# Attention block with compacted tokens: transfers regrouped, a row added to the reciprocals, buffers added

## The chip, the cores and the metric

The kernel runs on one core of a Trainium2 chip. The metric is the device time of one execution in microseconds (us). TensorE is called PE, VectorE DVE, ScalarE ACT, GpSimd POOL and SyncE SP, as in the profile.

## The reference

For each of 16 batches, with x of 512 features by 1024 tokens and a 0/1 mask over the tokens:

```python
xt = jnp.transpose(x, (0, 2, 1))
q = xt @ Wq.T                                   # 8 heads of 64
scores = scale * jnp.einsum('bhqd,bhkd->bhqk', qh, qh)
logits = (scores * cmask + (1.0 - cmask) * NEG) * rmask
attn = jax.nn.softmax(logits, axis=-1)
ctx = jnp.einsum('bhqk,bhkd->bhqd', attn, qh)
out = ctx @ Wo.T
return x + jnp.transpose(out, (0, 2, 1))
```

Queries, keys and values are one and the same projection. A masked query row has all logits zero, so its result is the mean of the values of all 1024 tokens. An unmasked row attends to unmasked tokens only.

## The kernel before, in words

For each batch the kernel works on C = 544 slots that hold the unmasked tokens (384 to 544 of them, which the kernel tests): four blocks of 128 and a tail of 32. Rows are fetched by gathers on POOL's queue (`rows`) and written back by scatters on it (`scatter_now`). Masked rows receive the mean of the values, added in `rest` (L742).

One batch goes through these steps. `xt` transposes the gathered rows on PE into a PSUM buffer `pm` (two of them) and splits them into two 16-bit parts (ACT L352, DVE L353). `query` projects (L414), ACT copies the result to `q` (L417), and DVE zeroes unused slots (L420). `qsplit` splits q of one pair of heads into a high part h and a low part l in the tile `hl` (L428, L429) and sends them by SP's queue into `xx`: for each head, the lower 64 partitions hold h and l, the upper ones l and h, so that one matmul over 128 rows sums two products. That takes six transfers a pair (L432 to L437), four pairs a batch. `value` transposes q to token order (L457, ACT L459, squares L448); `value_tail` does it for the tail (L474, DVE L477, which frees the `pm` buffer). `scores` multiplies xx with itself (L566), ACT takes the exponential with a row sum z (L570); the tails of four heads are done together (`i is None`, L545 to L560), and their high and low parts go to `pt` in four transfers. `attend` multiplies the exponentials by the values (L583, tails L586) and ACT copies the sum to `c` (L590).

`recip_sums` makes reciprocals of the row sums of a pair in columns of `rcol`: four blocks for each of two heads, and, for every second pair, a ninth column with the tail sums of four heads (zt). `recip_rows` transposes them (L620), DVE copies them to `rr` (L623), SP sends `rr` to a DRAM tile `rd` (L626) and from there, spread over 64 partitions each, into `rb`: per head 512 columns (L630) and 32 tail columns (L633), four transfers. `norm` multiplies c by rb (L655), adds means (L656) and splits the product into `ch` and `cl` (L658, L659) and the tail (L660, L661). `project` multiplies by the output weights (L671), DVE adds the row (`plus`, L676), and a scatter sends it.

The means need row sums of x in its own layout: `load_half` loads 128 x 512 pieces into two buffers `xm` by SP's queue (L337), eight a batch, and `sum_half` sums each on ACT (L343).

`run` sets the order. A batch has 18 steps (16 pairs of heads and blocks, and two tail steps); each step issues scores, then the functions due in `free`, then a share of the list `m`, which holds the next batch's `xt`, `query`, `value` and the last batch's `project`. `norm` of pair p is due five steps after the pair's last block; for pair 2 that is the batch's last step. Pair 3 follows in the next batch's list. This program order is a priority: a scheduler then orders each engine's instructions by it and by buffers, and every engine and SP's queue run in that fixed order, waiting on semaphores. An SP issue with an unmet wait holds up all issues behind it.

```python
for k in range(2 * DC):
    at = 3 * k // 2 + (0 if b else 4)
    free.setdefault(at, []).append(L(self.load_half, b + 2, k))
    free.setdefault(at + 3, []).append(L(self.sum_half, b + 2, k))
```

Of the kernel before, what the change touches and what calls it, by code (L numbers as in the profile page):

```python
# [49 lines left out]
class Fast:  # L50
# [12 lines left out]
    def __init__(self, ctx, tc, x, x_nat, mask_t, wq_t, wo_t, out):  # L63
        self.tc, self.nc = tc, tc.nc
        self.x, self.x_nat, self.out = x, x_nat, out
        self.B = x.shape[0] // T
        pool = lambda name, bufs, **k: ctx.enter_context(tc.tile_pool(name=name, bufs=bufs, **k))
        self.const = pool("const", 1)
        self.one = pool("one", 1)
        self.dram = pool("dram", 8, space=bass.MemoryType.DRAM)  # L70
        self.ps_s = pool("ps_s", 2, space=PS)
        self.ps_av = pool("ps_av", 1, space=PS)
        self.ps_m = pool("ps_m", 2, space=PS)
        self.st = {}
        self.scatters = []
        self.exp, self.pool = [], []

        self.paced, self.beat = False, None
        self.urgent, self.spare = [], []
        self.w, self.raw = {}, {}  # L80
        self.src = {"q": wq_t, "o": wo_t}
        self.setup(mask_t)
# [8 lines left out]
    def setup(self, mask_t):  # L91
# [25 lines left out]
        self.slot4 = iota("slot4", [P, 4], [[P, 4]], 0, 1)  # L117
# [5 lines left out]
        self.hit = fixed("hit", [P, B, 4])  # L123
        self.hit_t = fixed("hit_t", [P, B])
# [3 lines left out]
    def setup2(self):  # L128
# [11 lines left out]
        for t in self.rcol + self.smcol:  # L140
# [6 lines left out]

        self.tslot = fixed("tslot", [P, 1])
        t = self.sb([P, P], F32, "v", 6)
        nc.vector.tensor_tensor(t.rearrange("p (r t) -> p r t", r=HG), self.ident.rearrange("p (r t) -> p r t", r=HG),  # L150
                                self.row[:, 512 - NMIN:].unsqueeze(1).broadcast_to([P, HG, CT]), ALU.mult)
        nc.vector.tensor_reduce(self.tslot, t, AX.X, ALU.add)
# [62 lines left out]
    def facts(self, b0, b1):  # L215
# [6 lines left out]
        nc.vector.tensor_tensor(self.hit[:, bs], self.slot4.unsqueeze(1).broadcast_to([P, B, 4]),  # L222
                                n.unsqueeze(2).broadcast_to([P, B, 4]), ALU.is_lt)
        nc.vector.tensor_scalar(self.hit_t[:, bs], n, self.tslot, None, ALU.is_gt)
# [72 lines left out]

    def issue(self):
# [30 lines left out]
    def start(self, b):  # L329
        s = self.st[b] = {"xa": [], "xx": [], "v": [], "c": [], "nm": [], "corr": [], "rd": [], "xm": []}  # L330
        s["ms2"] = self.sb([P, 2 * DC], F32, "ms2", 2)
# [8 lines left out]
    def sum_half(self, b, k):  # L340
        s = self.st[b]
        with self.behind(*self.exp):
            self.nc.scalar.activation(s["xm"][k], s["xm"][k], AF.Copy, accum_out=s["ms2"][:, k:k + 1])  # L343

# [37 lines left out]
    def xt(self, b, k):  # L382
# [13 lines left out]
        if k == 4:  # L396
            ms = self.sb([P, DC], F32, "ms", 2)
            m = s["ms2"].rearrange("p (c h) -> p c h", h=2)
            with self.behind(s["at"]):
                nc.vector.tensor_tensor(ms, m[:, :, 0], m[:, :, 1], ALU.add)  # L400
            nc.vector.tensor_scalar(ms, ms, SX / T, None, ALU.mult)
# [20 lines left out]
    def qsplit(self, b, e):  # L422
# [4 lines left out]
        hl = self.sb([P, 2, C], F16, "hl", 1)  # L427
        nc.vector.tensor_copy(hl[:, 0, :], q)  # L428
        nc.vector.tensor_tensor(hl[:, 1, :], q, hl[:, 0, :], ALU.subtract)  # L429
        xx = self.sb([P, 4, C], F16, "xx", 5)  # L430
        lo, up = slice(0, DK), slice(DK, P)
        nc.sync.dma_start(out=xx[lo, 0:2, :], in_=hl[lo, :, :])  # L432
        nc.sync.dma_start(out=xx[up, 0, :], in_=hl[lo, 1, :])
        nc.sync.dma_start(out=xx[up, 1, :], in_=hl[lo, 0, :])  # L434
        nc.sync.dma_start(out=xx[lo, 2:4, :], in_=hl[up, :, :])
        nc.sync.dma_start(out=xx[up, 2, :], in_=hl[up, 1, :])
        nc.sync.dma_start(out=xx[up, 3, :], in_=hl[up, 0, :])  # L437
# [94 lines left out]
    def scores(self, b, p, i):  # L532
# [6 lines left out]
        if i is None:  # L539
# [16 lines left out]
            s["pt"] = self.sb([P, 2, C], F32R, "pt")  # L556
            half = slice(0, DK), slice(DK, P)
            for k in range(2):
                nc.sync.dma_start(out=s["pt"][half[k], k, :].bitcast(F32), in_=hi[half[k]].bitcast(F32))
                nc.sync.dma_start(out=s["pt"][half[1 - k], k, :].bitcast(F32), in_=lo[half[k]].bitcast(F32))  # L560
# [37 lines left out]
    def recip_sums(self, b, p):  # L598
# [4 lines left out]
        r = self.rcol[p % 2][:, :9]  # L603
        m = r[:, :8].rearrange("p (h k) -> p h k", k=4)
        k = 9 if p % 2 == 0 else 8
        nc.vector.tensor_tensor(m, s["z"][:, hs, :], corr[:, p % 2 * 2:p % 2 * 2 + 2].unsqueeze(2).broadcast_to([P, 2, 4]), ALU.subtract)
        if k == 9:
            nc.vector.tensor_tensor(r[:, 8:], s["zt"][:, g:g + 1], corr[:, HG:], ALU.subtract)
        nc.vector.tensor_scalar(r[:, :k], r[:, :k], 1e-35, 1.0 / SX, ALU.max, ALU.mult)
        nc.vector.reciprocal(r[:, :k], r[:, :k])  # L610
        nc.vector.tensor_tensor(m, m, self.hit[:, b, :].unsqueeze(1).broadcast_to([P, 2, 4]), ALU.mult)
        if k == 9:
            nc.vector.tensor_tensor(r[:, 8:], r[:, 8:], self.hit_t[:, b:b + 1], ALU.mult)

    def recip_rows(self, b, p):

        nc, s = self.nc, self.st[b]
        g, k = p // 2, 9 if p % 2 == 0 else 8
        pt = self.pm([P, P])
        nc.tensor.transpose(pt, self.rcol[p % 2], self.ident)  # L620
        rr = self.sb([9, P], F32, "rr", 2)
        with self.tc.high_priority(offset=HPO):
            nc.vector.tensor_copy(rr[:k], pt[:k])  # L623
        rd = self.dram.tile([9, P], F32, tag="rd", name="rd")
        s["rd"].append(rd)
        nc.sync.dma_start(out=rd[:k], in_=rr[:k])  # L626
        rb = self.sb([P, C], F32, "rb", 2)
        for k in range(2):
            half = slice(k * DK, (k + 1) * DK)
            nc.sync.dma_start(out=rb[half, :512],  # L630
                              in_=rd[4 * k:4 * k + 4, :].rearrange("k t -> (k t)").unsqueeze(0).broadcast_to([DK, 512]))
            t = (2 * p + k) % HG * CT
            nc.sync.dma_start(out=rb[half, 512:], in_=s["rd"][2 * g][8:9, t:t + CT].broadcast_to([DK, CT]))  # L633
        s.setdefault("rb", {})[p] = rb

    def norm(self, b, p):
# [4 lines left out]
        if p == 0:  # L641

            s["ch"] = self.sb([P, NP, 512], F16, "ch") if b < self.B - 1 else self.xh[:, :, :512]
            s["cl"] = self.sb([P, NP, 512], F16, "cl") if b < self.B - 1 else self.xl[:, :, :512]
# [120 lines left out]
    def last(self, b, todo):  # L765

        for f in todo:
            f()
        while self.urgent or self.spare:
# [20 lines left out]
    def run(self, flag):  # L790
# [81 lines left out]
        for b in range(B + 1):  # L872
# [8 lines left out]
            if n < B:  # L881
# [3 lines left out]
                for x in rests.get(b, []):  # L885
                    free.setdefault(0, []).extend(L(self.late, x, j) for j in range(5, 9))
                    late += [(0, L(self.rest, x, j)) for j in range(5, 9)]
            P_ = (lambda *i: project(o, *i)) if b else (lambda *i: [])
            tp, bt = [(0.1, L(self.top, b, 1))], [(0.1, L(self.bottom, b, 1))]
            if n < B:  # L890
                m = xt(n)[:1] + early[0] + xt(n)[1:3] + early[1] + xt(n)[3:] + tp + query(n, 0, 0) + query(n, 0, 1) + bt + value(n, 0)
# [13 lines left out]
            else:  # L905
# [7 lines left out]
                m = early[0] + early[1] + tp + bt + [(2.6, L(self.project_means, b))] + late + P_(0, 1, 2, 3)  # L913
# [11 lines left out]
            if b + 2 < B:  # L925
                self.start(b + 2)
                for k in range(2 * DC):
                    at = 3 * k // 2 + (0 if b else 4)
                    free.setdefault(at, []).append(L(self.load_half, b + 2, k))
                    free.setdefault(at + 3, []).append(L(self.sum_half, b + 2, k))  # L930
# [5 lines left out]
            for st, (p, i) in enumerate(S):  # L936
                for f in free.get(st, []):
# [30 lines left out]
                if i == 3:  # L968
                    (whole if p < 3 else todo).append(L(self.attend, b, p, 4, None))
                    if p < 3:  # L970
                        free.setdefault(st + 2, []).append(L(self.recip_sums, b, p))
                        free.setdefault(st + 3, []).append(L(self.recip_rows, b, p))
                        free.setdefault(st + 5, []).append(L(self.norm, b, p))
# [148 lines left out]
```

## Time and profile before

| what | value |
|---|---|
| median of three runs | 1149.91 us (1149.72 to 1152.34) |
| the profiled execution's time | 1141.3 us |
| its span, first to last instruction | 1139.4 us |
| mean granted PE clock | 0.992 |
| PE, DVE, ACT, POOL busy | 1090.1, 715.4, 685.4, 289.3 us |
| share of DMA engines: SP's queue q1, POOL's q0 | 35.6%, 18.9% |
| transfers issued on SP: xx, rb, xm, pt | 384, 256, 116, 128 |

PE's line is the one to watch. Busy time of the others lies beside it unless PE waits for them. In the totals of waits a row reads: engine, tile and line that waited, who released it, us in total, times, longest. In a stage's row come PE busy, PEld, DVE, ACT, POOL with counts, then the granted clock, the share of the DMA engines and GB/s.

### The profile page before, as it was taken

How to read it: one execution, taken by the hardware profiler on the slowest of the kernel's cores; microseconds unless marked ns; L12 is line 12 of the kernel's file. 1: busy time of each engine (PE TensorE's matmuls, PEld its weight loads, DVE VectorE, ACT ScalarE, POOL GpSimd, SP SyncE). 2: the span in 40 equal slices, each digit the busy share in tenths (PEclk: the TensorE clock that was granted, in tenths of full speed). 3: DMA queues.
4: the chain of work that ended last, by engine and by line, in shares of the span. 5: the costliest groups of instructions: out<-in, count | busy, mean ns of one | idle time of the engine just before them, and what ended most of it. 6: DMA issues, size and time to landing. Idle time of an engine off the chain costs nothing.

```text
span 1139.4 us, 23750 instructions
## 1 busy us (share of the span) xinstructions
PE 1090.1 (96%) x8386; PEld 705.5 (62%) x8386; DVE 715.4 (63%) x2262; ACT 685.4 (60%) x1828; POOL 289.3 (25%) x303
## 2 busy tenths in 40 slices
PE   7899999989999999999999999999999999999997
PEld 6566665656666566565666666666666666665553
DVE  7687477564656667576574766847576584655643
ACT  5876666556665666565666666666656666654550
POOL 3010121222202122232322223222222223214542
PEclk9999999999999999999999999999999999999999
DMA  7645455555545555555655565555655655445742
GB/s 233 197 140 145 132 156 159 172 132 161 150 128 157 152 177 152 163 163 146 180 146 171 158 186 158 156 173 155 183 160 149 187 143 158 137 131 164 218 151 88
DMA packets 106478, 181.35 MB, mean 159 GB/s; under 512 B 28096, under 2 KB 46176, under 8 KB 106352
## 3 DMA queue, kind: packets, MB, share of 16 engines
q1 hardware_dynamic: 85168, 111.59, 35.6%
q0 software_dynamic: 21184, 68.18, 18.9%
q8 instruction: 68, 1.11, 0.4%
q14 instruction: 58, 0.48, 0.1%
HBM read 92.34 MB, written 33.87 MB: 111 GB/s over the span
## 4 chain that ended last, share of the span: by engine, by line
PE 67%; DMA 12%; DVE 7%; issue 6%; SPq 5%; POOL 2%; ACT 1%; DVEq 0%; POOLq 0%; ACTq 0%
PE pav L583 18%; PE pss L566 15%; PE pm L671 12%; PE pm L414 12%; DMA xx<-hl 4%; DMA rb<-rd 4%; PE pav L586 2%; PE pm L392 2%; PE pm L457 2%; DMA xi<-x_in,idx 2%; PE pss L545 1%; SPq L630 1%; POOL y_out L755 1%; PE pm L620 1%; SPq L434 1%
## 5 line engine op out<-in xcount | busy, mean ns | idle before, releaser
L570 ACT ACTIVATE p<-pss,nm 128x544 f32<-128x544 f32 x512 | 364.3, 716 | 227.4 <-PE pss L566 217.0
L566 PE MATMUL pss<-xx 128*128 128x272 f16 x2048 | 304.1, 280 | 3.1 <-DMA xx<-hl 2.8
L583 PE MATMUL pav<-p,v 128*64 128x272 f32 x2048 | 301.4, 405 | 1.3 <-ACT c L590 1.3
L566 PEld LDWEIGHTS <-xx 128*128 128x128 f16 x2048 | 191.5, 99 | 84.6 <-issue 38.1
L583 PEld LDWEIGHTS pav<-p,v 128*64 128x64 f32 x2048 | 140.0, 137 | 107.1 <-issue 44.4
L414 PE MATMUL pm<-xh,wqh 128*128 128x274 f16 (+1 forms) x512 | 143.7, 281 | 1.0 <-DVE nm L510 0.9
L755 POOL DMA_INDIRECT y_out<-xa,idx x68 | 70.1, 1030 | 292.0 <-PE pss L566 171.8
L414 PE MATMUL pm<-xl,wqh 128*128 128x274 f16 (+1 forms) x512 | 143.3, 280 | 0.2 <-DVE xl L353 0.2
L414 PE MATMUL pm<-xh,wql 128*128 128x274 f16 (+1 forms) x512 | 143.4, 280 | 0.0
L313 POOL DMA_INDIRECT xa<-x_in,idx x68 | 70.0, 1029 | 173.9 <-DMA rb<-rd 39.8
L414 PEld LDWEIGHTS <-wqh 128*128 128x128 f16 x1024 | 99.1, 98 | 23.6 <-issue 4.9
L570 ACT ACTIVATION_READ_ACCUMULATOR p<-pss,nm 128x1 f32 x512 | 103.3, 202 | 0.0
L313 POOL DMA_INDIRECT xi<-x_in,idx x60 | 58.6, 977 | 164.0 <-PE pss L566 71.8
L655 DVE TENSOR_TENSOR c<-c,rb 128x544 f32<-128x544 f32 x64 | 46.3, 724 | 72.7 <-DMA rb<-rd 65.9
L671 PE MATMUL pm<-woh,cl 128*128 128x512 f16 x240 | 91.0, 379 | 0.0
L671 PE MATMUL pm<-wol,ch 128*128 128x512 f16 x240 | 90.9, 379 | 0.0
L671 PE MATMUL pm<-woh,ch 128*128 128x512 f16 x240 | 90.9, 379 | 0.0
L755 POOL DMA_INDIRECT y_out<-xi,idx x60 | 62.1, 1035 | 109.3 <-PE pss L566 99.7
L417 ACT ACTIVATE q<-pm 128x272 f32<-128x272 f32 (+1 forms) x128 | 51.3, 400 | 61.6 <-PE pm L414 60.9
L343 ACT ACTIVATE xm<-xm 128x512 f32<-128x512 f32 x116 | 73.4, 633 | 1.7 <-DMA xm<-x_nat_in 1.7
L676 DVE SCALAR_TENSOR_TENSOR xa<-pm,xa 128x512 f32<-128x512 f32 x60 | 41.3, 689 | 48.7 <-PE pm L671 48.5
L671 PEld LDWEIGHTS <-ch 128*128 128x128 f16 x480 | 46.1, 98 | 40.5
(194 smaller groups left out, 1550.8 us busy)
## 6 DMA issues: line engine op xcount, KB each, us to landing
xm<-x_nat_in SPq DMA_DIRECT2D x116, 256.0 KB
xx<-hl SPq DMA_DIRECT2D x256, 68.0 KB
xx<-hl SPq DMA_DIRECT2D x128, 136.0 KB
rb<-rd SPq DMA_DIRECT2D x128, 128.0 KB
pt<-c SPq DMA_DIRECT2D x64, 136.0 KB
pt<-p SPq DMA_DIRECT2D x64, 136.0 KB
ub<-ud SPq DMA_DIRECT2D x16, 256.0 KB
xi<-x_nat_in SPq DMA_DIRECT2D x8, 256.0 KB
```

The costliest lines, as they stand in the source:

```text
L313: dma = self.nc.gpsimd.indirect_dma_start(out=tile[:n], out_offset=None, in_=self.x, in_offset=bass.IndirectOffsetOnAxis(ap=idx, axis=0))
L343: self.nc.scalar.activation(s["xm"][k], s["xm"][k], AF.Copy, accum_out=s["ms2"][:, k:k + 1])
L392: self.pe = nc.tensor.transpose(pt[:, c, :], x[:n, c * P:(c + 1) * P], self.ident[:n, :n]).ins
L414: self.beat = nc.tensor.matmul(pq, lhsT=w[:, c, e * P:(e + 1) * P], rhs=xx[:, c, cols], start=(k == 0), stop=(k == 3 * DC - 1)).ins
L417: nc.scalar.activation(s["q"][:, e, cols], pq, AF.Copy, scale=1.0 / (SX * SW))
L566: self.beat = nc.tensor.matmul(pt[:, g, :CH], lhsT=xx[:, 2 * k, i * P:(i + 1) * P], rhs=xx[:, 2 * k + a, g * CH:(g + 1) * CH], start=(a == ...
L570: self.exp = [nc.scalar.activation(t.rearrange("p (g c) -> p g c", g=2), pt[:, :, :CH], AF.Exp, bias=s["nm"][p // HG][:, p % HG:p % HG + 1 ...
L583: nc.tensor.matmul(s["pav"][k * DK:(k + 1) * DK, g, :CH], lhsT=s["v"][p][:, i, k * DK:(k + 1) * DK], rhs=ps[k][:, cols], start=(i == 0), s ...
L655: nc.vector.tensor_tensor(c, c, s["rb"][p], ALU.mult)
L671: nc.tensor.matmul(po[:cols.stop - cols.start], lhsT=a[:, e, cols], rhs=w[:, e, :], start=(e == 0 and k == 0), stop=(e == DC - 1 and k == 2))
L676: self.nc.vector.scalar_tensor_tensor(x, po, 1.0 / (SX * SW), x, ALU.mult, ALU.add)
L755: dma = self.nc.gpsimd.indirect_dma_start(out=self.out, out_offset=bass.IndirectOffsetOnAxis(ap=idx, axis=0), in_=x, in_offset=None)
```

## The change

- `hl` gets a third plane that holds h again, so that [h, l] and [l, h] are each one block: four transfers of 136 KB a pair instead of two such and four of 68 KB. `hl` has two buffers instead of one.
- These transfers and the four of `pt` go through `later`, which keeps them to the beginning of the next step.
- The tail sums of a pair's two heads become a fifth row a head: two subtractions on 32 partitions each, ten columns for every pair. `rb` then comes in one transfer a head, 544 columns. `hit_t` and its setup go.
- From the third batch on, row sums are made of 128 x 1024 pieces: four loads and four sums a batch, sums four steps after the load.
- `ch` and `cl` have two buffers. `norm` of pair 2 moves into the next batch's list (`chunk2`), except in the last batch.

Per batch these are 40 plain transfers (16 xx, 4 pt, 4 pt in the second tail step, 4 rd, 8 rb, 4 xm) instead of 60.

```diff
+    def later(self, f):
+        if self.paced:
+            self.soon.append(f)
+        else:
+            f()
...
+    def load_all(self, b, c):
+        t = self.sb([P, T], F32, "xm", 2)
+        self.nc.sync.dma_start(out=t, in_=self.x_nat[b, c * P:(c + 1) * P, :])
+        self.st[b]["xm"].append(t)
...
-        hl = self.sb([P, 2, C], F16, "hl", 1)
+        hl = self.sb([P, 3, C], F16, "hl", 2)
         nc.vector.tensor_copy(hl[:, 0, :], q)
         nc.vector.tensor_tensor(hl[:, 1, :], q, hl[:, 0, :], ALU.subtract)
+        nc.vector.tensor_copy(hl[:, 2, :], hl[:, 0, :])
         xx = self.sb([P, 4, C], F16, "xx", 5)
-        lo, up = slice(0, DK), slice(DK, P)
-        nc.sync.dma_start(out=xx[lo, 0:2, :], in_=hl[lo, :, :])
-        nc.sync.dma_start(out=xx[up, 0, :], in_=hl[lo, 1, :])
-        nc.sync.dma_start(out=xx[up, 1, :], in_=hl[lo, 0, :])
-        nc.sync.dma_start(out=xx[lo, 2:4, :], in_=hl[up, :, :])
-        nc.sync.dma_start(out=xx[up, 2, :], in_=hl[up, 1, :])
-        nc.sync.dma_start(out=xx[up, 3, :], in_=hl[up, 0, :])
+        def spread():
+            lo, up = slice(0, DK), slice(DK, P)
+            nc.sync.dma_start(out=xx[lo, 0:2, :], in_=hl[lo, 0:2, :])
+            nc.sync.dma_start(out=xx[up, 0:2, :], in_=hl[lo, 1:3, :])
+            nc.sync.dma_start(out=xx[lo, 2:4, :], in_=hl[up, 0:2, :])
+            nc.sync.dma_start(out=xx[up, 2:4, :], in_=hl[up, 1:3, :])
+        self.later(spread)
...
-        if k == 9:
-            nc.vector.tensor_tensor(r[:, 8:], s["zt"][:, g:g + 1], corr[:, HG:], ALU.subtract)
+        for h in range(2):
+            q = (2 * p + h) % HG
+            rows = slice(q * CT, (q + 1) * CT)
+            nc.vector.tensor_tensor(m[:CT, h, 4:5], s["zt"][rows, g:g + 1], corr[rows, HG:], ALU.subtract)
...
         for k in range(2):
-            half = slice(k * DK, (k + 1) * DK)
-            nc.sync.dma_start(out=rb[half, :512],
-                              in_=rd[4 * k:4 * k + 4, :].rearrange("k t -> (k t)").unsqueeze(0).broadcast_to([DK, 512]))
-            t = (2 * p + k) % HG * CT
-            nc.sync.dma_start(out=rb[half, 512:], in_=s["rd"][2 * g][8:9, t:t + CT].broadcast_to([DK, CT]))
+            nc.sync.dma_start(out=rb[k * DK:(k + 1) * DK, :], in_=rd[5 * k:5 * k + 5, :].rearrange("k t -> (k t)")[:C]
+                              .unsqueeze(0).broadcast_to([DK, C]))
...
-            s["ch"] = self.sb([P, NP, 512], F16, "ch") if b < self.B - 1 else self.xh[:, :, :512]
-            s["cl"] = self.sb([P, NP, 512], F16, "cl") if b < self.B - 1 else self.xl[:, :, :512]
+            s["ch"] = self.sb([P, NP, 512], F16, "ch", 2) if b < self.B - 1 else self.xh[:, :, :512]
+            s["cl"] = self.sb([P, NP, 512], F16, "cl", 2) if b < self.B - 1 else self.xl[:, :, :512]
...
+            chunk2 = [(0, L(self.norm, o, 2))] if b else []
-                m = xt(n)[:1] + early[0] + xt(n)[1:3] + early[1] + xt(n)[3:] + tp + query(n, 0, 0) + query(n, 0, 1) + bt + value(n, 0)
+                m = xt(n)[:1] + early[0] + xt(n)[1:2] + chunk2 + xt(n)[2:3] + early[1] + xt(n)[3:] + tp + query(n, 0, 0) + query(n, 0, 1) + bt + value(n, 0)
...
-                for k in range(2 * DC):
-                    at = 3 * k // 2 + (0 if b else 4)
-                    free.setdefault(at, []).append(L(self.load_half, b + 2, k))
-                    free.setdefault(at + 3, []).append(L(self.sum_half, b + 2, k))
+                for c in range(DC):
+                    at = 3 * c + (0 if b else 4)
+                    free.setdefault(at, []).append(L(self.load_all, b + 2, c))
+                    free.setdefault(at + 4, []).append(L(self.sum_half, b + 2, c))
...
-                for f in free.get(st, []):
+                soon, self.soon = self.soon, []
+                for f in soon + free.get(st, []):
                     f()
...
-                        free.setdefault(st + 5, []).append(L(self.norm, b, p))
+                        if p < 2 or b == B - 1:
+                            free.setdefault(st + 5, []).append(L(self.norm, b, p))
```

## The prediction

> **What bounds the kernel now.** I read the page's first part, then the totals of waits, then one batch boundary in order of time. TensorE (PE) is the bound.
>
> ```profile
> PE 1090.1 (96%) x8386; PEld 705.5 (62%) x8386; DVE 715.4 (63%) x2262; ACT 685.4 (60%) x1828; POOL 289.3 (25%) x303
> ```
>
> The change leaves the matmuls as they are, so it can only win idle PE time: 1139.4 - 1090.1 = 49.3 us, of which 5.6 lie in the first 20 us and 8.0 after 1120 (stages of 20 us). What PE waits for in between is VectorE (DVE), and what DVE waits for is transfers (totals of waits: us, times, longest):
>
> ```profile
> PE pm L392 <- DVE tmp L477: 12.1, 10, 2.1
> PE pm L457 <- DVE q L420: 7.1, 7, 2.9
> DVE c L655 <- DMA rb<-rd: 65.9, 31, 4.2
> DVE hl L428 <- DMA xx<-hl: 37.2, 14, 3.4
> ```
>
> Ten times, once per batch boundary, the next batch's transpose (L392) waits for the value-tail multiply (L477) to free its PSUM buffer. One such boundary in order of time, DVE first, then SP's queue, then PE (start, duration, and in brackets the idle time before):
>
> ```profile
> 641.35 0.50 DVE L428 CAST hl<-q 128x544 f16<-128x544 f32 x1 [2.90 <-DMA xx<-hl]
> ...
> 647.04 0.73 DVE L655 TENSOR_TENSOR c<-c,rb 128x544 f32<-128x544 f32 x1 [1.47 <-DMA rb<-rd]
> ...
> 650.02 0.42 DVE L477 TENSOR_TENSOR tmp<-pm,par 128x256 f32<-128x256 f32 x1
> ```
> ```profile
> 638.85 0.43 SPq L626 DMA_DIRECT2D rd<-rr  x1
> 641.92 0.46 SPq L434 DMA_DIRECT2D xx<-hl  x1
> 642.47 0.55 SPq L630 DMA_DIRECT2D rb<-rd  x1
> 643.07 0.59 SPq L633 DMA_DIRECT2D rb<-rd  x1
> 643.72 0.59 SPq L630 DMA_DIRECT2D rb<-rd  x1
> 644.35 0.60 SPq L633 DMA_DIRECT2D rb<-rd  x1
> ```
> ```profile
> 648.13 0.62 PE L566 MATMUL pss<-xx 128*128 128x272 f16 x4
> 648.68 0.67 PE L583 MATMUL pav<-p,v 128*64 128x272 f32 x2
> 650.49 0.66 PE L392 MATMUL pm<-ident,xa 128*128 128x128 f32 x4 [1.14 <-DVE tmp L477]
> ```
>
> DVE sits 2.90 us because the only `hl` buffer is still being read by six transfers. The cast then releases the xx issue L434, which stands in SP's queue ahead of four rb issues about 0.64 us apart. The last starts at 644.35 and its wait ends at 647.04, 2.69 later. Norm starts there, and L477 stands 2.98 us of work behind it. PE loses 1.14.
>
> **The change, part by part** (line numbers of the kernel before).
>
> *hl in two buffers.* At this boundary the cast could start at 638.45, 2.90 earlier. *Six xx issues become four, four rb issues two.* In the built order of the changed kernel the rb issues stand behind two xx issues of the new hl, and the second needs the third plane. So SP reaches the last rb at: cast 0.50 + subtract 0.73 + copy 0.3 + two xx issues 1.2, less 0.5 because the first xx starts during the copy, + one rb issue 0.64 = about 2.9 after the cast's start. Before it was 644.35 - 641.35 = 3.00. The shorter list only pays for the third plane; the gain is the earlier cast. Counting from 638.45 the last rb could start at 641.4. But rd, issued at 638.85, must land first: the chain shows 2.01 us for one, so 640.9, and I allow until 642.0 for the last rb. It lands 2.69 later, 644.7: 2.3 us earlier than 647.04. Norm also stands behind the product's `plus` (L676), which PE releases and which ends at 643.90; no limit. L477 therefore comes up to 2.3 earlier. I take 1.9, since the tail sums and ten-column reciprocals stand around there. Ends: 1.0 (the rd landing and xx gating take the rest) and 2.9 (all of it).
>
> Against this PE arrives earlier. In the built order the second transpose stands one pss matmul behind the first in these ten boundaries. Before, four pss and part of a pav group lay between. Three pss at 0.116 (L566, 0.93 us per eight) and two pav at about 0.12 make 0.6 us less cover. So 1.9 - 0.6 = 1.3 us is closed per boundary. The ten gaps are 2.08, 1.06, 1.19, 0.77, 0.78, 1.14, 0.68, 1.86, 1.43, 1.12 (sum 12.1); what exceeds 1.3 is 0.78 + 0.56 + 0.13 = 1.5. **Gain 10.6** (ends 4.0 and 12.1). Moving norm of pair 2 into the next batch's list does nothing by itself: the built order has it 11 DVE instructions ahead of L477, as against 10.
>
> *Six other PE gaps* have a wait for rb shortly before them on DVE: 1.89 at 82.7, 0.87 at 177.4, 1.23 at 443.4, 0.34 at 718.4, 1.30 at 1061.8, 1.65 at 1103.4; sum 7.3. I take half, **3.6** (ends 0 and 7.3).
>
> *The clock.* Behind four gaps PE ran 3.4 us at half clock, 1.7 lost each. Stages of such a stretch and of the gap before the second one:
>
> ```profile
> 236.80:240.20 3.40, 3.40 (x15) 1.49 (x13) 1.57 (x8) 2.38 (x7) 0.93 (x1) 0.50 0.20 58
> 523.00:526.00 3.00, 0.46 (x4) 0.41 (x5) 1.44 (x6) 0.28 (x3) 0.00 (x0) 1.00 0.80 171
> 526.90:530.30 3.40, 3.40 (x17) 1.76 (x16) 2.52 (x11) 1.31 (x5) 0.64 (x1) 0.50 0.73 188
> ```
>
> (Third number from the right: granted clock.) The gaps are 2.08, 2.70, 1.86 and 1.93 us; a gap of 2.90 at 249 brought none. The Trainium skill, "TensorE: Matmul & The Clock Gate" (section "Why this matters for your kernels"), asks only that gaps stay under about 3 us. By it none of these gaps costs clock and the change wins nothing here. By the rows two of four follow L477 gaps, worth 3.4. The rows decide, but 2.90 without a drop[...]: **2.0**.
>
> *L457 <- q (7.1) stays.* Its two large cases, 2.90 at 249 and 2.70 at 523, stand behind L742 waiting for an xi gather on POOL's queue. Nothing there is edited: 0, ends -2 and +2.
>
> *Third hl plane.* 64 copies f16 to f16, an operation no row shows. The same shape from f32 is 452 ns (L428): 29 us of DVE. By the Trainium skill, "VectorE: DVE Perf Modes" ("Side-by-side: where the cycles go"), four elements a cycle and 150 to start make an estimate of 0.30 us: 19 us. I take 0.3. A rule that speaks against the change is in "SBUF — State Buffer" (the trap in which DVE blocks DMA): such copies can lock GpSimd out while it writes descriptors. If each held a gather for its full length, gathers would run 19 us late in all, and the xi waits grow. But 64 L428 casts and 60 L658 casts run already, and all 60 xi gathers take 924 to 1273 ns. I book 0. *Recip:* 128 tail subtractions of 32x1 in place of 64 one-column operations at 0.15 (L608, L613): +10 us of DVE. Both lie in DVE's 424 idle us, except where DVE is full (17.8 of 20 us at 440-460, 18.9 at 720-740, 17.7 at 920-940): **-1.0** (ends 0 and -3).
>
> *Sums in one piece.* ACT: 112 x (633 + 203) ns = 94 us become 56 x (1061 + 203) = 71; 1061 is 633 plus 512 elements at 0.84 ns (L444: 629 for 512, 415 for 256). ACT waits 217 us for PE at L570 anyway: 0. Cost if that cover fails: an exponential 0.43 us late. SP waits 93.5 us at the sum's buffer (L337) now; with loads two steps after the sums that frees it become rarer. It hides in SP's slack and is in the 1.9.
>
> *Deferral to the next step* (about 68 us of a batch in 18 steps, 3.8 us): xx is not used until the next batch; the built order keeps its issues right behind hl. pt is used three steps on: 11.4 - 3.8 = 7.6 us against four issues and a landing, 4 x 0.6 + 2.7 = 5.1. L586 waits 0.3 for pt now: 0. *ch and cl twice:* L658 waits 6.6 us in all for PE and no PE wait lies behind: 0. *Start:* the first xx issues stand behind two more weight loads, and the third plane is needed: **-0.5** (PE's wait there is 2.85 now; ends +0.6 and -1.5).
>
> Sum: 10.6 + 3.6 + 2.0 - 1.0 - 0.5 = **14.7 us**. The profiled execution took 1141.3 us (span 1139.4), so 1126.6. The runs' median is 8.6 above it; I carry that over: 1149.9 - 14.7 = 1135.2, say **1136**. All low ends together give about 0, all high ends about 25.
>
> **The rivals.** *A, bursts of sums (smaller gain).* Each load is now 512 KB, and two stand ahead of pair 0's xx and rd. At 270 GB/s (the fastest 20 us stage) the extra 512 KB is 1.9 us. Pair 0's rb waits are 1.15 to 4.18 us now and none of them stalls PE. With 1.9 more, what exceeds 4.18 sums to 9.7 us over 14 batches: 1149.9 - 14.7 + 9.7 = 1145. Against it: two issues fewer, and an earlier rd.
>
> *B, slower.* At the boundaries PE has 0.6 us less cover. If rb still lands as late, because it now waits for the third plane and two xx, each of ten gaps grows by 0.6, and one or two more pass the 1.9 us at which the clock dropped: 6 + 2 x 1.7 less what the six others give, about 1156. It decides where L477 comes less than 0.6 us earlier. For it: the 2.9 against 3.0 above. Against it: the 37.2 us of hl waits have their cause removed.
>
> *C, no change.* Another wait is right behind: L448 waits 42.7 us for ACT's v, xi stays. L477 is then released by ACT instead and gains and losses cancel: 1149. Against: v is ready near 647.2 at this boundary, while L448 starts at 649.42.
>
> *D, more.* All DVE-caused gaps go, xi waits shrink with fewer packets in the way: 25 us, 1125.
>
> **How the numbers follow.** Forecast 0.53, A 0.15, B 0.13, C 0.12, D 0.07. A run can tell about 0.3%, 3.4 us. Faster: forecast, D, and most of A: 0.73. Same: C and the rest of A: 0.14. Slower: 0.13. The forecast's own range is 1129 to 1144; with A and C, half of B, and the edge of D it is 1127 to 1154.
>
> **What would show it.** DVE's wait of hl for xx near 0; waits of c for rb at pair 2 under 1 us (now 1.0 to 2.2); PE's wait for L477 (then L487) under 3 us; PE's idle time 49 to about 36; two stretches at half clock instead of four; q waits about 7. Wrong if rb waits at pair 2 stay, or L392 waits despite them, or pair 0's rb waits pass 5 us and PE stops behind them.

## The result and the profile after

| | before | changed |
|---|---|---|
| median (lowest to highest) of four runs each | 1151.12 us (1149.72 to 1153.78) | 1135.16 us (1133.48 to 1137.83) |
| profiled execution, span | 1141.3, 1139.4 us | 1133.56, 1131.8 us |
| granted clock in it | 0.992 | 0.992 |
| PE idle within the span | 49.3 us | 41.3 us |

The ratio of the changed kernel to the one before is 0.9866, with the interval 0.982 to 0.9911: 16.0 us faster, where 13.9 was forecast (1149.9 to 1136). But the two profiled executions lie only 7.7 us apart, so half of what was measured is not in them, and a longer series on another chip (e7 below) gives 0.9921, about 9 us. All three figures are taken up below.

The first part of the page of the changed kernel, busy time by engine and the DMA packets:

```profile
PE 1090.5 (96%) x8386; PEld 707.9 (63%) x8386; DVE 731.6 (65%) x2369; ACT 676.2 (60%) x1716; POOL 289.1 (26%) x303
...
DMA packets 78122, 181.35 MB, mean 160 GB/s; under 512 B 15008, under 2 KB 16800, under 8 KB 78000
```

PE does the same work. DVE has 107 instructions and 16 us more, ACT 112 and 9 us less. The totals of waits, PE's and then DVE's:

```profile
PE pm L633 <- DVE rcol L627: 5.8, 5, 2.1
PE pm L633 <- DVE m L511: 5.0, 7, 1.0
PE pm L467 <- DVE q L427: 4.1, 5, 1.8
...
PE pm L633 <- DVE rcol L624: 1.3, 2, 0.7
PE pm L398 <- DVE tmp L487: 1.3, 2, 0.8
```
```profile
DVE xa L685 <- PE pm L680: 89.5, 43, 7.4
DVE c L664 <- DMA rb<-rd: 42.5, 29, 3.7
```

The wait at the batch boundaries (now L398 for L487) went from 12.1 us to 1.3, and DVE's wait for the `hl` buffer (37.2 us) is gone. In their place stands a wait that was small before: the transpose of the reciprocals (L633, before L620) waits 12.1 us in all for DVE, before 6.7.

The same boundary as in the prediction, in order of time, SP's queue, DVE and PE:

```profile
631.49 0.60 SPq L445 DMA_DIRECT2D xx<-hl  x1
632.19 0.48 SPq L638 DMA_DIRECT2D rd<-rr  x1
634.42 0.46 SPq L442 DMA_DIRECT2D xx<-hl  x1
634.97 0.55 SPq L443 DMA_DIRECT2D xx<-hl  x1
635.88 1.11 SPq L641 DMA_DIRECT2D rb<-rd  x2
```
```profile
633.15 0.43 DVE L435 CAST hl<-q 128x544 f16<-128x544 f32 x1
...
638.55 0.69 DVE L685 SCALAR_TENSOR_TENSOR xa<-pm,xa 128x512 f32<-128x512 f32 x1 [3.49 <-PE pm L680]
640.18 0.72 DVE L664 TENSOR_TENSOR c<-c,rb 128x544 f32<-128x544 f32 x1 [0.93 <-DMA rb<-rd]
...
643.39 0.42 DVE L487 TENSOR_TENSOR tmp<-pm,par 128x256 f32<-128x256 f32 x1
```
```profile
643.86 0.65 PE L398 MATMUL pm<-ident,xa 128*128 128x128 f32 x4
```

The cast waits for nothing, the two rb issues (one row, x2) go out from 635.88, and the second L398 starts without a wait. The first two lines matter below: the last xx issue of the pair before, and rd right behind it. In the kernel before, `plus` and the xx issue right ahead of rd (638.85) were:

```profile
643.22 0.68 DVE L676 SCALAR_TENSOR_TENSOR xa<-pm,xa 128x512 f32<-128x512 f32 x1
```
```profile
638.27 0.46 SPq L437 DMA_DIRECT2D xx<-hl  x1
```

Measured against the start of `plus` (L685), which PE paces, norm (L664) starts 1.63 us later; before it was 3.82. So it comes 2.2 us earlier, where the prediction had up to 2.3 and took 1.9. What the earlier cast freed, though, DVE now spends in the 3.49 us before `plus`.

### The profile page after: what moved, and what is told of

Same layout as the page of the kernel before. It is cut to its first block, busy times and chain, and to the rows that moved or that the text cites. A ratio compares the mean times of both kernels' runs of the same rounds, so it can differ in the third digit from the quotient of the medians.

```text
span 1131.8 us, 23296 instructions
## 1 busy us (share of the span) xinstructions
PE 1090.5 (96%) x8386; PEld 707.9 (63%) x8386; DVE 731.6 (65%) x2369; ACT 676.2 (60%) x1716; POOL 289.1 (26%) x303
## 2 busy tenths in 40 slices
DMA packets 78122, 181.35 MB, mean 160 GB/s; under 512 B 15008, under 2 KB 16800, under 8 KB 78000
## 3 DMA queue, kind: packets, MB, share of 16 engines
q1 hardware_dynamic: 56816, 111.62, 35.6%
## 4 chain that ended last, share of the span: by engine, by line
PE 66%; DVE 14%; DMA 11%; issue 5%; ACT 2%; POOL 1%; SPq 1%; DVEq 0%; POOLq 0%; ACTq 0%
PE pav L597 19%; PE pss L580 16%; PE pm L680 13%; PE pm L421 8%; DMA rb<-rd 4%; PE pm L398 2%; DMA rd<-rr 2%; PE pav L600 2%; DMA xi<-x_in,idx 2%; PE pm L467 1%; DVE c L664 1%; DMA xx<-hl 1%; PE pm L633 1%; DVE tmp L458 1%; PE pss L555 1%
## 5 line engine op out<-in xcount | busy, mean ns | idle before, releaser
L597 PE MATMUL pav<-p,v 128*64 128x272 f32 x2048 | 297.5, 402 | 0.9 <-ACT c L604 0.9
L685 DVE SCALAR_TENSOR_TENSOR xa<-pm,xa 128x512 f32<-128x512 f32 x60 | 41.4, 689 | 89.6 <-PE pm L680 89.5
L664 DVE TENSOR_TENSOR c<-c,rb 128x544 f32<-128x544 f32 x64 | 46.2, 722 | 49.2 <-DMA rb<-rd 42.5
L751 DVE TENSOR_TENSOR xi<-xi,ub 128x512 f32<-128x512 f32 (+1 forms) x60 | 40.1, 687 | 40.2 <-DMA xi<-x_in,idx 27.7
```

What stands on the lines that cost most here:

```text
L597: nc.tensor.matmul(s["pav"][k * DK:(k + 1) * DK, g, :CH], lhsT=s["v"][p][:, i, k * DK:(k + 1) * DK], rhs=ps[k][:, cols], start=(i == 0), s ...
L664: nc.vector.tensor_tensor(c, c, s["rb"][p], ALU.mult)
L685: self.nc.vector.scalar_tensor_tensor(x, po, 1.0 / (SX * SW), x, ALU.mult, ALU.add)
L751: self.nc.vector.tensor_tensor(x[:n], x[:n], s["ub"][:n], ALU.add)
```

## Where PE's idle time went

All PE gaps of 0.25 us and more, sorted by the prediction's terms. The first pair is the two profiles above. The second is one more profile of each kernel, unedited, from another chip (the last of the experiments below). Gains are positive.

| term | predicted | first pair | second pair |
|---|---|---|---|
| batch boundaries (L477, now L487) | 10.6 | 12.1 - 1.3 = 10.8 | 12.4 - 2.5 = 9.9 |
| six other gaps | 3.6 | 7.3 - 3.0 = 4.2 | 3.0 - 3.3 = -0.3 |
| q behind an xi gather, near 252 and 525 | 0 | 5.6 | 5.3 |
| third plane and fifth row on DVE | -1.0 | -7.9 | -8.6 |
| start, first 60 us | -0.5 | -2.5 | -2.7 |
| around 1035 to 1045 | none | -1.5 | -0.7 |
| sum of gaps | 12.7 | 8.7 | 2.9 |

The sums are those of the gaps; the profiled executions themselves lie 7.7 and 3.7 us apart. The boundary term held in both pairs, the six other gaps only in the first, and three terms in neither. The largest miss is on DVE. It stands at one place a batch, where PE transposes reciprocals shortly after the next batch's q. First that place in the kernel before, DVE and PE, then in the changed one:

```profile
354.09 0.32 DVE L420 TENSOR_TENSOR q<-q,hr 128x160 f32<-128x160 f32 x1
...
355.75 0.29 DVE L501 TENSOR_REDUCE m<-pm 128x1 f32<-128x128 f32 x1
```
```profile
355.45 0.27 PE L499 MATMUL pm<-ident,smcol 128*128 128x128 f32 x1
...
356.10 0.33 PE L620 MATMUL pm<-ident,rcol 128*128 128x128 f32 x1
```
```profile
354.18 0.32 DVE L427 TENSOR_TENSOR q<-q,hr 128x160 f32<-128x160 f32 x1
...
354.62 0.15 DVE L624 TENSOR_TENSOR rcol<-zt,corr 32x1 f32<-32x1 f32 x1
...
355.28 0.72 DVE L436 TENSOR_TENSOR hl<-q,hl 128x544 f16<-128x544 f32 x1
355.91 0.30 DVE L437 COPY hl<-hl 128x544 f16<-128x544 f16 x1
356.12 0.17 DVE L627 TENSOR_TENSOR rcol<-rcol,hit 128x10 f32<-128x10 f32 x1
356.30 0.15 DVE L624 TENSOR_TENSOR rcol<-zt,corr 32x1 f32<-32x1 f32 x1
356.38 0.27 DVE L511 TENSOR_REDUCE m<-pm 128x1 f32<-128x128 f32 x1
```
```profile
355.33 0.27 PE L509 MATMUL pm<-ident,smcol 128*128 128x128 f32 x1
...
356.71 0.33 PE L633 MATMUL pm<-ident,rcol 128*128 128x128 f32 x1 [0.67 <-DVE m L511]
```

The transpose needs a `pm` buffer that the small reduction to `m` frees. Before, DVE reached L501 as PE's product L499 ended (355.45 + 0.27 = 355.72), and the transpose went straight on. Now the copy L437 and tail subtractions L624 stand in the same row of DVE work, which has no pause there. From q's mask to the reduction it is 2.20 us instead of 1.66, and PE waits 0.67. Between 150 and 970 us of the span PE waits at L633 eleven times, mostly at this place, 0.64 to 1.01 us each: 7.85 us together, where L620 had no wait at all.

## The experiments

Times are medians of 8 to 10 runs (e3: four, e8: one) against 22 to 31 runs of the kernel before on the same chip. Executions of one kernel differ by about 1% with the granted clock, so a second figure stands beside each: the mean of the time less (1 - clock) x span, an estimate of the time at full clock, for which the runs of one kernel spread by 0.7 to 3.0 us (standard deviation). Sets, each on one chip: e1 to e4; e5 to e8; e9 to e12. The medians of the kernel before in them are 1148.6, 1144.5 and 1144.7 us; the ratio comes with its interval from the single runs and is not the quotient of these medians.

| run | median us | ratio (interval) | clock | at full clock: before, this |
|---|---|---|---|---|
| e1 before, hl twice | 1144.3 | 0.9938 (0.9908 to 0.9968) | 0.9877 | 1132.6, 1129.1 |
| e2 changed, hl once | 1138.8 | 0.9919 (0.9891 to 0.9947) | 0.9898 | 1132.6, 1126.3 |
| e3 changed, six xx | 1136.5 | 0.9892 (0.9841 to 0.9944) | 0.9912 | 1132.6, 1127.7 |
| e4 changed, half sums | 1138.4 | 0.9911 (0.9882 to 0.9940) | 0.9905 | 1132.6, 1127.0 |
| e5 before, fifth row | 1137.6 | 0.9955 (0.9923 to 0.9987) | 0.9918 | 1130.7, 1128.9 |
| e6 changed, four rb | 1141.8 | 0.9973 (0.9942 to 1.0004) | 0.9916 | 1130.7, 1132.0 |
| e7 changed | 1134.0 | 0.9921 (0.9891 to 0.9951) | 0.9909 | 1130.7, 1125.0 |
| e9 tail sums early | 1142.5 | 0.9989 (0.9962 to 1.0016) | 0.9915 | 1131.5, 1132.5 |
| e10 norm not moved | 1135.6 | 0.9924 (0.9894 to 0.9953) | 0.9916 | 1131.5, 1126.0 |
| e11 not deferred | 1134.8 | 0.9928 (0.9902 to 0.9954) | 0.9922 | 1131.5, 1125.6 |
| e12 ch, cl once | 1134.9 | 0.9923 (0.9894 to 0.9952) | 0.9902 | 1131.5, 1124.0 |

**e1: the second `hl` buffer alone, in the kernel before.**

```diff
-        hl = self.sb([P, 2, C], F16, "hl", 1)
+        hl = self.sb([P, 2, C], F16, "hl", 2)
```

> The kernel before, with a second hl buffer and nothing else. Theory hl (the second buffer frees VectorE at the batch boundary, and that is most of the gain): DVE's wait of hl for xx goes from 37 us to under 5, PE's wait for L477 from 12.1 us to under 5, the time is 8 to 12 us below before, ratio 0.990 to 0.993. Theory issues (fewer issues on SP's queue are what brings rb earlier): the hl waits go, but rb lands as late as before, L477 still holds PE 9 us or more, ratio 0.997 to 1.000. Theory sums (SP's queue freed of the waits for the sums' buffers): ratio 0.998 to 1.000.

Waits of PE in e1:

```profile
PE pm L392 <- DVE tmp L477: 8.2, 8, 2.8
```

DVE's wait for `hl` is gone from the totals, and the boundaries keep 8.2 of 12.1 us. The earlier cast alone closes a third of them, between what the two theories said (under 5, 9 or more). The time at full clock falls by 3.5 us, about as much as these waits.

**e2: the changed kernel with one `hl` buffer.**

```diff
-        hl = self.sb([P, 3, C], F16, "hl", 2)
+        hl = self.sb([P, 3, C], F16, "hl", 1)
```

> The changed kernel with one hl buffer. Theory hl: the boundary waits come back, and the third plane makes them longer; PE waits for L487 10 us or more; 9 to 15 us above the changed kernel, 0.995 to 1.003 of before. Theory issues: four issues instead of six also shorten the wait for the single buffer; no more than 4 us above the changed kernel, 0.987 to 0.991. Theory sums: as the changed kernel, 0.986 to 0.989.

The same boundary in e2, SP and DVE:

```profile
635.34 1.10 SPq L641 DMA_DIRECT2D rb<-rd  x2
636.62 0.48 SPq L442 DMA_DIRECT2D xx<-hl  x1
```
```profile
635.35 0.45 DVE L435 CAST hl<-q 128x544 f16<-128x544 f32 x1 [0.97 <-DMA xx<-hl]
...
639.63 0.72 DVE L664 TENSOR_TENSOR c<-c,rb 128x544 f32<-128x544 f32 x1
```

DVE waits 24.4 us for `hl` again, and the boundaries still lose only 2.9. In this build the rb issues stand ahead of the new pair's xx issues at all ten boundaries, so a late cast does not hold them up, and here norm finds rb landed. At full clock e2 lies 6.3 us below the kernel before, the changed kernel 5.7 below it on another chip (e7): beside the rest of the change, no gain of the second buffer can be told from zero.

**e3: the changed kernel with six xx transfers and no third plane**, hl still twice.

```diff
-        hl = self.sb([P, 3, C], F16, "hl", 2)
+        hl = self.sb([P, 2, C], F16, "hl", 2)
...
-        nc.vector.tensor_copy(hl[:, 2, :], hl[:, 0, :])
...
-            nc.sync.dma_start(out=xx[up, 0:2, :], in_=hl[lo, 1:3, :])
+            nc.sync.dma_start(out=xx[up, 0, :], in_=hl[lo, 1, :])
+            nc.sync.dma_start(out=xx[up, 1, :], in_=hl[lo, 0, :])
...
```

> The changed kernel with two planes of hl (two buffers) and six xx transfers a pair again; rb, sums and the rest as changed. Theory hl: within 3 us of the changed kernel on either side, 0.984 to 0.990, since the shorter list only pays for the third plane. Theory issues: 6 us or more of the gain is lost, 0.992 to 0.997, with waits of c for rb at the boundaries back to 1 to 2 us. Theory sums: as the changed kernel.

Its profiled execution (1143.45 us), waits of PE:

```profile
PE pm L398 <- DVE tmp L488: 9.6, 9, 2.4
PE pm L634 <- DVE rcol L628: 7.4, 5, 2.3
PE pm L634 <- DVE m L512: 3.6, 8, 0.6
```

The profile says that without the shorter xx list most of the boundary waits are back, though the cast is early. But this execution is not typical of the kernel: at full clock it took 1132.0 us, the other three 1125.3 to 1127.2, as fast as the changed kernel. So whether the runs lose what this profile shows stays open. The last row is clearer: the wait at the reciprocals is 0.43 us a time (eight of the eleven between 150 and 975 us) instead of 0.67, with only the copy missing on DVE.

**e4: row sums in half pieces again.**

```diff
-                for c in range(DC):
-                    at = 3 * c + (0 if b else 4)
-                    free.setdefault(at, []).append(L(self.load_all, b + 2, c))
-                    free.setdefault(at + 4, []).append(L(self.sum_half, b + 2, c))
+                for k in range(2 * DC):
+                    at = 3 * k // 2 + (0 if b else 4)
+                    free.setdefault(at, []).append(L(self.load_half, b + 2, k))
+                    free.setdefault(at + 3, []).append(L(self.sum_half, b + 2, k))
...
```

> The changed kernel with the loads and sums of x in halves again, eight of each a batch. Theory hl and theory issues: within 3 us of the changed kernel, 0.984 to 0.990. Theory sums: SP's queue waits for the sums 90 us again, rb comes later, and 5 us or more of the gain is lost, 0.991 or above. If the long loads hurt (rival A of the prediction), this one is 3 us or more faster than the changed kernel, 0.983 or below.

Boundaries 2.1 us, L633 12.6: like the changed kernel. At full clock it is 5.6 us below the kernel before, as e7 is 5.7 below it on its chip. The large pieces give and cost nothing that could be told.

**e5: the fifth row and one rb transfer a head, in the kernel before** (`recip_sums`, `recip_rows` and the setup of `hit` from the changed kernel).

```diff
-            nc.sync.dma_start(out=rb[half, :512], ...)
-            nc.sync.dma_start(out=rb[half, 512:], ...)
+            nc.sync.dma_start(out=rb[k * DK:(k + 1) * DK, :], in_=rd[5 * k:5 * k + 5, :]...)
```

> The kernel before with the fifth row and one rb transfer a head, and nothing else of the change. Theory rb issues (what counts is when the last rb transfer is issued, and norm stands behind a PE-gated plus that hides the hl wait): two issues of 0.64 us fewer bring rb 1.3 us earlier at the boundaries; PE's wait for L477's multiply falls from 12.1 us to 4 us or less, the ratio is 0.990 to 0.994, as good as or better than the second hl buffer alone (0.9938). Theory hl: the hl waits of 37 us stay and hold the boundary; PE waits 9 us or more for that multiply, ratio 0.997 to 1.001.

Waits of PE in e5:

```profile
PE pm L384 <- DVE tmp L469: 9.7, 10, 2.5
...
PE pm L611 <- DVE m L493: 3.4, 9, 0.4
```

Two rb issues less close 2.4 of the 12.1 us: the theory of the rb issues, which had 4 us or less left, fails when this edit stands alone. And a wait appears that the kernel before does not have: 0.37 to 0.39 us, nine times, at the place shown above. The fifth row brings it, without any third plane. This edit alone also has 0.52 and 0.35 us where the kernel before waits 2.90 and 2.70 for q behind an xi gather.

**e6: the changed kernel with rb in four transfers.**

```diff
-            nc.sync.dma_start(out=rb[k * DK:(k + 1) * DK, :], in_=...[:C]...)
+            flat = rd[5 * k:5 * k + 5, :].rearrange("k t -> (k t)")
+            nc.sync.dma_start(out=rb[k * DK:(k + 1) * DK, :512], in_=flat[:512]...)
+            nc.sync.dma_start(out=rb[k * DK:(k + 1) * DK, 512:], in_=flat[512:C]...)
```

> The changed kernel with rb in four transfers a pair again (512 and 32 columns from the five rows). Theory rb issues: rb comes 1.3 us later at the boundaries, PE's wait for L487's multiply rises from 1.3 to 7 us or more, 4 to 9 us above the changed kernel, ratio 0.991 to 0.995. Theory hl: within 2 us of the changed kernel, ratio 0.986 to 0.990, that wait under 4 us.

Waits of PE in e6:

```profile
PE pm L633 <- DVE rcol L627: 14.6, 14, 2.9
PE pm L398 <- DVE tmp L487: 5.4, 5, 2.6
```

This edit costs 7.8 us by the medians of e6 and e7, 7.0 at full clock: the whole gain. But only part of that stands at the boundaries. Of 5.8 us more in PE's gaps than in e7, 2.9 are waits for L487 (5.4 us, between the two theories' under 4 and 7 or more), 2.0 are at the reciprocals (15.2 against 13.2 in all), and the rest is scattered. The scheduler also put 815 of DVE's 2369 instructions in another order than in the changed kernel, so the 7.8 us cannot be put down to two issues alone.

**e7 and e8: both kernels again, unedited**, for the scatter of the profiles. e8 had one run, 1137.7 us.

> The changed kernel, unedited, for its time and granted clock beside the others of this call and for a second profile. Theory clock (about half of the gain is less time at half clock): its mean granted clock is 0.003 to 0.006 above that of the kernel before, which at 1.15 us for each 0.001 is 3.5 to 7 us of a difference of 12 to 16; ratio 0.986 to 0.990. Theory waits alone: the clocks agree within 0.002 and the whole difference is PE's waits. Start of the second batch near 82 us as in the first profile if the later start belongs to the change or to the chip.

> The kernel before, unedited, for a second profile. Theory clock: the first profile, at clock 0.992, was one with few stretches at half clock; this one shows six or more of them and a clock near 0.986, with a time 6 to 8 us above 1141. If the later start of the second batch (82.6 us in the changed kernel against 75.8) belongs to the execution and not to the change, this profile has it near 82 too; if it belongs to the change, near 76.

The waits repeat: 12.4 us for L477 in e8, 2.5 for L487 in e7. The gain does not repeat in size: 10.5 us between the medians here, 16.0 at first. That the clock does this is likely but not shown, since the first runs of the kernel before have no clock on record. Both theories of the clock fail: e7's mean clock is 0.0023 above that of the kernel before, and not 0.003 to 0.006; e8 has four stretches at half clock and a mean clock of 0.991, where six or more and 0.986 were expected. e8 is a quick execution, 3.2 us below the mean of its kernel at full clock, so the second pair of profiles shows too little of the gain. In 25 and 10 runs the mean time falls by 8.5 us (1143.8 to 1135.3), of which 5.7 at full clock, and 2.6 by the clock (0.9886 to 0.9909, times 1135).

**e9: tail subtractions early**, meant to take them off the way to L633.

```diff
+            def tails():
+                for q in range(HG):
+                    rows, h = slice(q * CT, (q + 1) * CT), q % 2
+                    nc.vector.tensor_tensor(self.rcol[q // 2][:CT, 5 * h + 4:5 * h + 5], s["zt"][rows, p:p + 1],
+                                            s["corr"][p][rows, HG:], ALU.subtract)
+            self.later(tails)
...
-        for h in range(2):
-            ...
```

> The changed kernel with the tail subtractions moved out of the reciprocals' chain: all four of a group right after its tail exponentials, in the next step. Theory chain (the new PE waits for the transposed reciprocals, L633, 12 to 14 us in the changed kernel against 5 to 7 before, come from two more DVE operations in that chain): those waits fall by 3 us or more, the time is 2 to 5 us below the changed kernel, ratio 0.984 to 0.991. Theory place (they come from where PE's order puts the transpose): the waits stay within 2 us, the time within 2 us.

Waits of PE in e9:

```profile
PE pm L467 <- DVE q L427: 9.8, 15, 1.8
PE pm L636 <- DVE m L511: 8.5, 11, 1.2
```

It went the other way: the wait at the transpose is 0.84 us a time instead of 0.67, q's waits grow by 5, and the gain is gone (7.7 us slower than e11). The scheduler also put other instructions in another order (227 of DVE's 2369), so the 7.7 us cannot be put down to four subtractions alone.

**e10, e11, e12: norm of pair 2 at its old step; no deferral; `ch` and `cl` once.**

```diff
-            chunk2 = [(0, L(self.norm, o, 2))] if b else []
+            chunk2 = [(0, L(self.norm, o, 2))] if b == B - 1 and False else []
...
-                        if p < 2 or b == B - 1:
+                        if True:
```
```diff
     def later(self, f):
-        if self.paced:
-            self.soon.append(f)
-        else:
-            f()
+        f()
```
```diff
-            s["ch"] = self.sb([P, NP, 512], F16, "ch", 2) if b < self.B - 1 else self.xh[:, :, :512]
+            s["ch"] = self.sb([P, NP, 512], F16, "ch") if b < self.B - 1 else self.xh[:, :, :512]
```

> The changed kernel with norm of pair 2 back at the batch's last step. Theory of the prediction (this move does nothing by itself): within 2 us of the changed kernel, PE's wait for L487's multiply under 4 us. Theory order (the move is what puts the transposes and norm so that PE does not wait): that wait 6 us or more and 4 us or more lost.

> The changed kernel with the xx and pt transfers issued at once, not in the next step. Theory of the prediction (deferral costs and gains nothing): within 2 us of the changed kernel. Theory queue (at once, the new xx issues stand in SP's queue ahead of rd and rb): waits of c for rb grow by 10 us or more over 37 to 43, PE waits for L487 6 us or more, 4 us or more lost. Should the start of the second batch (82 us against 76 to 78) come from the deferral, it is back under 79 here.

> The changed kernel with one buffer each of ch and cl. Theory of the prediction (their waits were hidden): within 2 us of the changed kernel. Theory buffers (with the earlier DVE, pair 0's norm now meets the products that still read ch): DVE waits for PE at ch of 15 us or more and 3 us or more lost.

All three give the changed kernel's time within the intervals. e12 shows a large wait that costs nothing (waits of DVE):

```profile
DVE ch L667 <- PE pm L680: 46.4, 14, 3.6
```

PE's wait for L487 is 1.9 us in it, 3.2 in e10 and 3.1 in e11. No version here beats the changed kernel beyond its interval.

## Why the prediction came out, step by step

*The boundaries: size right, reason wrong.* 10.6 us were predicted; 10.8 and 9.9 were found. But the step said "the shorter list only pays for the third plane; the gain is the earlier cast". That failed. Here are the means over the ten boundaries, read from each trace, in us from the start of `plus` (minus is before it), and PE's waits for the value-tail multiply in all:

| kernel | cast | rd issued | last rb issued | norm | PE waits |
|---|---|---|---|---|---|
| before | -2.0 | -4.8 | 1.0 | 3.9 | 12.1 |
| e5 before, fifth row, two rb | -2.0 | -5.2 | -0.3 | 3.1 | 9.7 |
| e1 before, hl twice | -5.5 | -5.0 | 0.2 | 3.0 | 8.2 |
| e3 changed, six xx | -5.4 | -4.9 | -1.4 | 2.4 | 9.6 |
| e6 changed, four rb | -5.4 | -6.3 | -0.6 | 2.3 | 5.4 |
| changed | -5.4 | -6.5 | -2.1 | 1.6 | 1.3 |
| e2 changed, hl once | -2.8 | -6.7 | -2.4 | 1.3 | 2.9 |

What the prediction missed is that the xx list stands ahead of rd too. The copy to `rr` ends 8.3 us before `plus` in the kernel before and 8.2 in the changed one, but rd must wait on SP for the xx issues of the pair before: six put it at -4.8, four at -6.5, and six in the changed kernel (e3) at -4.9. The first rb follows rd by 3.9 us before and after, at the boundary shown by 3.69; the prediction had 2.0 for rd's landing. From the first rb issue to the last it is 1.9 us with four and 0.5 with two. So the last rb goes out 3.0 us earlier, 1.7 by the earlier rd and 1.3 by the two issues fewer. The early cast alone (e1) brings it 0.8. In the changed order it keeps the two xx issues ahead of rb out of the way; where the order puts rb ahead of them (e2), it isn't needed. Of these 3.0 us 0.75 are lost again: the last rb transfer now has 136 KB and not 8, and norm starts 3.6 us after its issue instead of 2.9 (e6, with 8 KB last again, 2.9). That leaves 2.3 us, the prediction's own upper figure, by another sum. e3's PE waits do not fit the row of the others; its profiled execution is the untypical one.

*Six other gaps: 3.6 was 4.2 and -0.3.* They are 7.3 and 3.0 us in two profiles of the kernel before, so neither figure says much.

*The third plane and the fifth row on DVE: -1.0 was -7.9 and -8.6.* The prices were right: the copy took 0.29 to 0.30 us, as the prediction estimated from the Trainium skill's page "VectorE: DVE Perf Modes" ("Side-by-side: where the cycles go"), and not the 0.45 of the f32 row; a subtraction took 0.15. The cover was wrong. "DVE's 424 idle us" is a sum over the span, and the stages of 20 us were too coarse to show the 2 us in which DVE has no pause and PE stands right behind it. Step by step the wait there is 0 before, 0.37 with the fifth row (e5), 0.43 in the changed kernel without the copy (e3) and 0.67 with it: so about 0.24 for the copy, near what it occupies (355.91 to 356.12, 0.21).

*q behind xi: 0 was +5.6 and +5.3.* The prediction gave this ends of -2 and +2. In the changed kernel only one of the two xi additions stands before q's mask there: L751 at 250.42 and q at 251.32, and the second gather is issued at 251.12. The built order had moved it; the prediction read that order for the boundaries alone. The fifth row with one rb transfer a head is enough to move it: in e5 the second addition stands behind q (254.41 and 252.22) and the gaps are 0.52 and 0.35 us. In e1 they stay, 2.80 and 2.32. So the edit that costs at the reciprocals brings this gain by the order that it makes, which the prediction did not have.

*Start: -0.5 was -2.5 and -2.7*, in small gaps: three of about 0.5 us near 50 us that wait for ACT, and the rest at the first gather, q and, in the second pair, the first xx. Without deferral (e11) the first value-tail multiply of the second batch starts at 81.3 us, in the changed kernel at 82.6 and 82.3, in the kernel before at 75.8 and 78.1: deferral is not the main cause. What is, stays open.

*Clock and median: two errors that cancel.* Of the sum 14.7, the pair of profiles shows 7.7. The prediction then carried over 8.6 us by which the median of before lies above its profiled execution. For the changed kernel this is only 1.6 (1135.16 to 1133.56). The profiled execution of before had a clock of 0.992; the means of the later sets are 0.986 to 0.989, so runs at its usual clock lose more. So the forecast met the number partly by luck: 1135.2 was 7 us too optimistic on the gaps and the clock of the profiles, and as much too pessimistic on the runs around them. Against the longer series of e7, 8.5 us by the means, 13.9 is too much. The clock term of 2.0 is 2.6 in that series, and cannot be seen in the first profiles, where both kernels have 0.992: the two half-clock stretches behind L477 gaps are gone, as foreseen, but the changed kernel has others in its first 42 us, and in both PE worked 13.6 us at half clock. Nor does the clock follow the boundary gaps: in e5, with 9.7 us of them left, it is 0.0032 above the kernel before.

*Costed at nothing, and found so:* norm's move (e10), deferral (e11), `ch` and `cl` (e12), sums in one piece (e4). The copies did not visibly hold up the gathers either: DVE's waits for xi gathers went from 30.4 us to 27.7, and the 60 gathers take 924 to 1385 ns (before 924 to 1273).

*The signs.* `hl` waits near 0 and L487 under 3 us came. The rb waits at pair 2, to be under 1 us, are 0.25 to 1.67, and six of the thirteen are above. PE's idle time fell to 41.3, not 36. Stretches at half clock while PE worked are three instead of four, not two, and as long in sum. q's waits, to be about 7, are 4.1.

*The rivals.* A (512 KB loads hold up pair 0) fell: pair 0's rb waits are 0 to 3.67 us, before 1.15 to 4.18, and e4 without them gains nothing. B (slower) and C (no change) fell by the result. D came in one point, the xi waits.

## What to carry to other kernels

An engine with 35% idle time is no cover for a new instruction: look at the two microseconds before each instruction of the bound engine that it releases, and price the new work there, times the number of batches. On a queue that issues in order, follow the chain back: count the issues ahead of the transfer that is waited for, and those ahead of the transfer that this one needs (here rd). Neither an earlier cast alone (e1) nor fewer rb issues alone (e5) emptied the gaps. A profiled execution and a median differ by the clock of the runs, so compare profile with profile, and median with median, over many runs. And a small edit can change the order that a scheduler makes: look whether it did before putting a difference down to the edit.

## What the runs showed of the hardware

- PE ran at half clock in stretches of 3.4 or 6.8 us, behind gaps from 1.66 us (e9, at 460.65) to 3.37 us (e3, at 36.70), but not behind gaps of 1.76 and 2.24 (e7), 2.90 (before, at 251.96) and 3.17 us (e5, at 14.83). In these runs the length of a gap between 1.7 and 3.4 us does not tell whether it will cost clock.
- The mean granted clock ran from 0.984 to 0.994 between 25 executions of the kernel before on one chip (the set of e5 to e8), with times from 1152.0 to 1137.4 us; a straight line through them gives about 1.15 us for each 0.001.
- DMA packets fell by 27% (106478 to 78122), and those under 512 B from 28096 to 15008. The busy share of SP's queue stayed at 35.6%, with 111.6 MB on it: fewer packets hardly shortened the transfers in sum.
- From the start of the last rb issue to the end of its wait it was 3.79 us at the boundary shown (636.39, the second of the two, to 640.18), before 2.69; over the ten boundaries 3.6 and 2.9. Merging the transfers saved issue time, not landing time.
